# The last column block of 20 rows contracted as a block of 128, in a two-layer graph network on one core

## The chip, the cores and the metric

One Trainium2 chip, one of its cores. The metric is the device time of one execution in microseconds (us), the median of several runs. All data are float32. The engines have the names of the profile: PE is TensorE with its weight loads as PEld, DVE is VectorE, ACT is ScalarE, POOL is GpSimd, SP is SyncE, which here only issues DMAs.

## The reference

x is 2708 x 256, adj is 2708 x 2708 and sparse (about 0.3% filled, with a diagonal). Cut to what matters:

```
def layer0(x, adj, W, b):
    s = concatenate([x, adj @ x], axis=1)
    return layernorm(x + relu(s @ W + b))

def layer1(X, S, W1, W2, W3, U1, U2):
    R = (S + eye) / rowsum(S + eye)
    Xf = Xa = X; Z = 0
    for n in range(2):
        A  = top_p_attention(Xa, W1, W2, W3)   # softmax of q k^T, smallest set of mass 0.9, renormalized
        Xf = R @ Xf
        Xa = A @ Xa
        Z  = Z + Xf @ U1[n].T + Xa @ U2[n].T
    return layernorm(X + layernorm(X + Z))
```

2708 is 21 x 128 + 20, so a sum over all 2708 columns of adj, or of the attention matrix A, falls into 21 column blocks of 128 and a last one of 20.

## The kernel before

Rows are handled in NB = 22 blocks of P = 128, the last (EDGE = 21) with 20 rows. The order of instructions on every engine is that of the program text (a hand-written schedule); each engine takes its queue in that order. Tiles that the engines exchange are guarded by semaphores that the framework sets from the reads and writes of each region.

Layer 0 (L447 on). First y0 = x @ W[256:] is made for all blocks (L388 to L399) with a column of ones behind it at index D = 256, so that the row sum of adj comes along. Then for each row block m, `adj_product` (L247) adds up 22 products over the column blocks k in one PSUM tile: the stationary operand is a 128 x 128 piece of adj transposed, from the two loaded halves in `adj_of`, the moving one y0[:, k] of 257 columns. For k = 21 both have kw = 20 rows (partitions). The host sends adj as 128 x 128 blocks, filled with zeros beyond 2708. Then come x @ W[:256] (L462), the transposes of x1 (L438) and, every fourth block, the query and key projection (L426). On DVE the block has `name_columns` (L289), bias, relu and layernorm (L471 to L479) and, from block 16 on, rounds of list building (`lists.take`, L321 and L322).

`lists.end()` (L324 on) follows the loop of layer 0. DVE prepares a list, POOL stores it (L334), loads it back (L335), and DVE makes offsets of it (L339 to L341). POOL then sends seven scattering DMAs (L345), one after the other, and a load of the table ix (L348).

Next, attention step 1. Ahead of its loop, `begin1` makes the logits of blocks 0 to 2 (PE L507, ACT copy L514) with projections `u1_project` between (PE L651, ACT L654), `extract1` on DVE draws the 64 largest logits of a row (L570 to L579), `exps1` on ACT takes exponentials (L611, L613), and `finish1` on DVE finds and applies the threshold (L627 to L640). Then for each block t, in six groups of four column blocks, `turn` (L521) transposes the masked exponentials e to the tile wT (PE L527, ACT copies L530 and L533), and `products` (L553) multiplies wT with y (PE L564), one group later; y is x1 in step 1. The last group has two column blocks, k = 20 and k = 21, and k = 21 has 20 columns: a transpose of 20 columns, a separate ACT copy of 20 partitions (L533) and a product with 20 rows. Block 21, with 20 rows of its own, has its products in four column strips (L561), folded by `edge_sum` (L236).

Attention step 2 (from about 745 us) has the same `turn` and `products` with y = ya, which is Xa @ U2[1].T, made by `ya_pair` (L662) in pairs of blocks. Its row block 21 goes through `edge_product` (L536 on: PE L544, ACT L546, PE L550). Beside it run the sparse products of R (`r_units`, PE L749) with the gathered rows yg that POOL's indirect DMAs bring (`y_load`, L719), the threshold search on ACT (L966, L969) and DVE (L1023 to L1090), and the final layernorms.

e has NW = 2720 columns; those from 2708 on are set to zero at the start (L181). `y_room` (the tile yg) is 5416 columns wide; its first 4096 hold gathered rows, the next 1024 four spare tiles.

The forms to follow in the code are these:

```
nc.tensor.transpose(tr[:kw, k % 4, :p], e[:p, k * P:k * P + kw], ident[:p, :p])          # L527
nc.tensor.matmul(acc[:p, :D], lhsT=wT[:kw, k % 4, :p], rhs=y[:kw, k, :],                # L564
                 start=k == 0, stop=k == NB - 1)
nc.tensor.matmul(acc[:p, :n], lhsT=halves[k // KH][:kw, k % KH, :p], rhs=y[:kw, k, :n],  # L257
                 start=k == 0, stop=stop and k == NB - 1)
```

Of the kernel before, what the change touches and what calls it, by code (L numbers as in the profile page):

```python
# [20 lines left out]
P = 128  # L21
CH = 512
SEG = 170
NS = 16
# [14 lines left out]
CAP = 160  # L39
ML = 16  # L40
CW, CC = 128, 7


def chunks(N):
# [8 lines left out]
def gnn_two_layer_kernel(ctx: ExitStack, tc: tile.TileContext, N, xT_d, x_d, adj_d, w0_d, b0_d,  # L53
# [24 lines left out]
    nc = tc.nc  # L78
    D = x_d.shape[1]
    DA = w1_d.shape[1]  # L80
    NB = (N + P - 1) // P
    DC = D // P
    assert N % 2 == 0 and NB % 2 == 0 and N * 2.0 ** -15 < 0.09 and DC == 2 and DA == 64
    assert SEG * (NS - 1) + 8 <= N <= SEG * NS == SEG2 * NS2 and N >= SEG2 * (NS2 - 1) + 8
    assert NB == 3 * KS + 1 and CW == P and CAP % 8 == 0 and N < NB * P
    CHS = chunks(N)
    KH = NB // 2
# [61 lines left out]
def fast_path(ctx, tc, c, flags, fint, xT_d, x_d, w0_d, b0_d, w1_d, w2_d, w3_d, u1_d, u2_d, g_d, b_d):  # L149
    nc = tc.nc  # L150
    N, D, DA, NB, DC, KH, CHS, rows = c.N, c.D, c.DA, c.NB, c.DC, c.KH, c.CHS, c.rows
    ident = c.ident
# [94 lines left out]
    def adj_product(acc, m, y, n, stop):  # L247
        p = rows(m)
        halves = adj_of.pop(m)
        for k in range(NB):  # L250
            kw = rows(k)
            if m == EDGE:
                o = EW * (k % 4)
                nc.tensor.matmul(acc[o:o + p, :n], lhsT=halves[k // KH][:kw, k % KH, :p], rhs=y[:kw, k, :n],
                                 start=k < 4, stop=k >= NB - 4)
                continue
            nc.tensor.matmul(acc[:p, :n], lhsT=halves[k // KH][:kw, k % KH, :p], rhs=y[:kw, k, :n],  # L257
                             start=k == 0, stop=stop and k == NB - 1)


# [123 lines left out]
    adj_load(0, 0)  # L384
    adj_load(0, 1)
    y0 = big.tile([P, NB, D + 1], FP, tag="V", name="y0")
    nc.gpsimd.memset(y0[:, :, D:D + 1], 1.0)
    for t in range(NB):  # L388
        p = rows(t)
# [99 lines left out]
    YW = 2 * (CC + 1) * D  # L489
    yg = y_room[:, :YW].rearrange("p (s c d) -> p s c d", s=2, d=D)  # L490
    spares = [y_room[:, YW + D * i:YW + D * (i + 1)] for i in range(4)]
    lists = Lists(ML, NB, flags[:, NF - 2:], yg[:, 1].rearrange("p c d -> p (c d)"))
    lists.turn()
    x1_transpose(NB - 1)
# [23 lines left out]
    NG = (NB + 3) // 4  # L518
    before = []

    def turn(t, g, y, acc, e):  # L521
        p = rows(t)
        ks = range(4 * g, min(NB, 4 * g + 4))
        tr = ps_tr()
        for k in ks:
            kw = rows(k)
            nc.tensor.transpose(tr[:kw, k % 4, :p], e[:p, k * P:k * P + kw], ident[:p, :p])  # L527
        wT = work.tile([P, 4, P], FP, tag="wT", name="wT", bufs=3)
        full = sum(rows(k) == P for k in ks)
        nc.scalar.copy(wT[:, :full, :p], tr[:, :full, :p])  # L530
        if full < len(ks):
            kw = rows(ks[full])
            nc.scalar.copy(wT[:kw, full, :p], tr[:kw, full, :p])  # L533
        before.append((p, ks, wT, y, acc))

    def edge_product(y, acc, e):  # L536

        p = rows(EDGE)
        tr = ps_tr().rearrange("p k i -> p (k i)")[:, :NB * p].rearrange("p (k i) -> p k i", i=p)
        wT = work.tile([P, 4, P], FP, tag="wT", name="wT", bufs=3)  # L540
        wT = wT.rearrange("p k i -> p (k i)")[:, :NB * p].rearrange("p (k i) -> p k i", i=p)
        for k in [NB - 1] + list(range(NB - 1)):
            kw = rows(k)
            nc.tensor.transpose(tr[:kw, k, :], e[:p, k * P:k * P + kw], ident[:p, :p])  # L544
        for a, b, kw in ((0, NB - 1, P), (NB - 1, NB, rows(NB - 1))):
            nc.scalar.copy(wT[:kw, a:b, :], tr[:kw, a:b, :])  # L546
        for k in range(NB):
            kw = rows(k)
            o = EW * (k % 4)
            nc.tensor.matmul(acc[o:o + p, :D], lhsT=wT[:kw, k, :], rhs=y[:kw, k, :],  # L550
                             start=k < 4, stop=k >= NB - 4)

    def products(keep):  # L553

        if len(before) > keep:
            p, ks, wT, y, acc = before.pop(0)
            for k in ks:
                kw = rows(k)
                if p < P:
                    o = EW * (k % 4)  # L560
                    nc.tensor.matmul(acc[o:o + p, :D], lhsT=wT[:kw, k % 4, :p], rhs=y[:kw, k, :],  # L561
                                     start=k < 4, stop=k >= NB - 4)
                    continue
                nc.tensor.matmul(acc[:p, :D], lhsT=wT[:kw, k % 4, :p], rhs=y[:kw, k, :],  # L564
                                 start=k == 0, stop=k == NB - 1)

    def seg_max(dst, src, p, step, width):
# [94 lines left out]
    def ya_pair():  # L662
# [11 lines left out]
        if rows(t0 + 1) == P:  # L674
            nc.scalar.copy(ya[:, t0:t0 + 2, :], pz)
            return
        for s in range(2):
            nc.scalar.copy(ya[:rows(t0 + s), t0 + s, :], pz[:rows(t0 + s), s, :])

    def step1_out(t, acc, ra):  # L680

# [215 lines left out]
    for t in range(NB):  # L897
# [6 lines left out]
        for g in range(NG):  # L904
# [16 lines left out]
            if g == 2:  # L921
                if t + 3 < NB:
                    extract1(t + 3)
                if t < 9:
                    lists.take(2 * t + 2, 2 * t + 4)
                if t == 8:
                    lists.end()
            if (t, g) in at:
                adj_gather(at[t, g])
                stores += [(NG * t + g + i, at[t, g], i - 4) for i in (4, 5)]  # L930
# [804 lines left out]
```

## Time and profile before

| | |
|---|---|
| median of 3 runs | 1295.33 us (1294.3 to 1296.72) |
| the profiled execution | 1291.2 us; span of its instructions 1289.4 us; mean granted PE clock 0.986 |
| PE busy | 1226.3 us, 95% |
| DVE busy | 973.9 us, 76% |
| ACT busy | 735.5 us, 57% |
| POOL busy | 635.9 us, 49% |
| L564, L257 matmuls (passes) | 924 on x and 924 on ya at L564, 924 at L257 |
| ACT copies at L530 (all forms) | 258, 132.1 us |

Every float32 product shows as two passes, each with a weight load (PEld), so 924 is 2 x 21 x 22. A form such as 20*128 20x256 gives the rows and columns of the stationary operand, then partitions and columns of what moves. A PE row of the timeline ends late, since the ends of pipelined matmuls are modelled: the distance from start to start is what a pass costs. "Idle before" with a releaser says what ended the wait; "issue" means that the profile shows nothing that it waited for.

The chain of work that ended last is 79% PE, 8% DVE, 7% ACT, 3% DMA and 2% POOL.

### The profile page before, as it was taken

To read this page: it belongs to the slowest core of one execution; us is meant where nothing else is said; L and a number is where in the kernel's file an instruction comes from. 1 tells how busy PE (TensorE), PEld (TensorE's weight loads), DVE (VectorE), ACT (ScalarE), POOL (GpSimd) and SP (SyncE) were. 2 spreads that over 40 slices of the span, in tenths; PEclk is the share of its full clock that TensorE was granted. 3 is DMA by queue.
4 is the path that set the end of the run, shared out by engine and by line. 5 is a ranking of instruction groups with operands and counts; after the bars stand their busy time and mean duration, and the time that the engine had idled before them with its cause. 6 is when DMAs were issued, how large, how long until landed. Compare 5 with 4: busy or idle time off the path is not lost.

```text
span 1289.4 us, 18741 instructions
## 1 busy us (share of the span) xinstructions
PE 1226.3 (95%) x5764; PEld 888.1 (69%) x5764; DVE 973.9 (76%) x3252; ACT 735.5 (57%) x1337; POOL 635.9 (49%) x594
## 2 busy tenths in 40 slices
PE   8999999979899999999999987999999999999885
PEld 6878777843477777777777555777766777767664
DVE  2445545884999997977872179889888999999886
ACT  2000110125456656556655488887888989989822
POOL 1000000003475452577756058878874878888860
PEclk9999999999999999999999988999999999999998
DMA  7455445423322210122224244565563545565451
GB/s 196 152 193 170 143 149 168 149 90 107 121 82 83 72 57 28 43 88 91 93 85 100 63 149 150 178 189 177 180 154 118 179 155 154 165 195 158 145 139 39
DMA packets 101703, 165.99 MB, mean 129 GB/s; under 512 B 17362, under 2 KB 74070, under 8 KB 101594
## 3 DMA queue, kind: packets, MB, share of 16 engines
q1 hardware_dynamic: 75308, 108.65, 26.0%
q0 software_dynamic: 20544, 51.17, 14.3%
q10 hardware_dynamic: 5742, 4.89, 1.3%
q8 instruction: 48, 0.79, 0.2%
q14 instruction: 61, 0.50, 0.1%
HBM read 130.74 MB, written 33.90 MB: 128 GB/s over the span
## 4 chain that ended last, share of the span: by engine, by line
PE 79%; DVE 8%; ACT 7%; DMA 3%; POOL 2%; issue 2%; ACTq 0%; POOLq 0%; DVEq 0%
PE acc L564 27%; PE acc L257 16%; PE lg L507 9%; PE misc L749 8%; PE tr L527 7%; PE acc L651 2%; DMA yg<-v_d,ix 2%; PE acc L462 2%; PE misc L392 2%; PE misc L426 2%; PE acc L672 2%; ACT e L966 2%; PE misc L699 1%; DVE e L1088 1%; ACT e L844 1%
## 5 line engine op out<-in xcount | busy, mean ns | idle before, releaser
L530 ACT COPY wT<-tr 128x512 f32<-128x512 f32 (+2 forms) x258 | 132.1, 519 | 208.7 <-PE tr L527 208.7
L564 PE MATMUL acc<-x,wT 128*128 128x256 f32 (+1 forms) x924 | 230.5, 388 | 0.0
L564 PE MATMUL acc<-ya,wT 128*128 128x256 f32 (+1 forms) x924 | 227.1, 385 | 0.0
L719 POOL DMA_INDIRECT yg<-v_d,ix x154 | 194.8, 1265 | 59.6 <-issue 22.6
L564 PEld LDWEIGHTS acc<-x,wT 128*128 128x128 f32 (+1 forms) x924 | 165.2, 189 | 71.0 <-issue 37.4
L719 POOL DMA_INDIRECT yg<-yf_d,ix x154 | 188.2, 1222 | 48.3 <-issue 22.5
L257 PE MATMUL acc<-y,adj_t 128*128 128x257 f32 (+1 forms) x924 | 208.4, 381 | 0.0
L564 PEld LDWEIGHTS acc<-ya,wT 128*128 128x128 f32 (+1 forms) x924 | 170.2, 190 | 44.4 <-issue 24.0
L749 PE MATMUL misc<-yg,adj_t 128*128 128x256 f32 (+1 forms) x704 | 183.7, 394 | 14.9 <-DMA yg<-v_d,ix 5.9
L367 POOL DMA_INDIRECT adj_t<-in_adj,ix x154 | 171.3, 1112 | 52.0 <-issue 41.8
L257 PEld LDWEIGHTS acc<-y,adj_t 128*128 128x128 f32 (+1 forms) x924 | 171.8, 189 | 32.7 <-issue 8.9
L749 PEld LDWEIGHTS misc<-yg,adj_t 128*128 128x128 f32 (+1 forms) x704 | 123.6, 189 | 67.6 <-issue 23.4
L507 PE MATMUL lg<-k,q 64*128 64x512 f32 (+3 forms) x528 | 149.5, 594 | 13.7 <-ACT e L848 7.0
L527 PE MATMUL tr<-ident,e 128*128 128x128 f32 (+2 forms) x946 | 147.1, 274 | 3.1 <-DVE e L1088 2.0
L527 PEld LDWEIGHTS tr<-ident,e 128*128 128x128 f32 (+2 forms) x946 | 112.2, 138 | 44.8 <-issue 16.4
L334 POOL DMA_DIRECT2D part_d<-e x1 | 0.6, 573 | 285.6 <-DVE e L333 285.6
L439 ACT COPY x1T<-tr 128x256 f32<-128x256 f32 (+1 forms) x22 | 8.0, 364 | 186.6 <-PE tr L438 186.6
L966 ACT ACTIVATE e<-e,st 128x2708 f32<-128x2708 f32 (+1 forms) x43 | 113.5, 2639 | 0.1
L969 ACT ACTIVATE e<-e,st 128x2708 f32<-128x2708 f32 (+1 forms) x42 | 110.9, 2641 | 0.1
L570 DVE MAX8 cand<-e 128x8 f32<-128x170 f32 (+1 forms) x352 | 87.2, 318 | 26.7 <-ACT e L514 26.7
L1030 DVE MAX8 cand<-w 128x8 f32<-128x170 f32 (+1 forms) x352 | 94.2, 321 | 0.0
L1083 DVE MATCH_REPLACE8 w<-part,e 128x680 f32<-128x680 f32 (+1 forms) x88 | 74.3, 851 | 0.0
(238 smaller groups left out, 1696.4 us busy)
## 6 DMA issues: line engine op xcount, KB each, us to landing
adj_t<-in_adj SPq DMA_DIRECT2D x44, 704.0 KB
adj_t<-adjc_d SPq DMA_DIRECT2D x44, 448.0 KB
adjc_d<-adj_t SPq DMA_DIRECT2D x22, 256.0 KB
base<-za_d SPq DMA_DIRECT2D x40, 128.0 KB
adjc_d<-adj_t SPq DMA_DIRECT2D x22, 192.0 KB
xt<-in_x ACTq DMA_DIRECT2D x21, 128.0 KB
x_d<-x SPq DMA_DIRECT2D x21, 128.0 KB
x1b_d<-xb SPq DMA_DIRECT2D x21, 128.0 KB
```

The source lines that it names most:

```text
L257: nc.tensor.matmul(acc[:p, :n], lhsT=halves[k // KH][:kw, k % KH, :p], rhs=y[:kw, k, :n], start=k == 0, stop=stop and k == NB - 1)
L367: nc.gpsimd.indirect_dma_start(out=a[:CW, i, :], out_offset=None, in_=adj_rows, in_offset=bass.IndirectOffsetOnAxis(ap=ix[:CW, m, i:i + 1] ...
L507: nc.tensor.matmul(lg[:p, h, :b - a], lhsT=q[o, t * P:t * P + p], rhs=keys[s][o, i, :b - a], start=True, stop=True)
L527: nc.tensor.transpose(tr[:kw, k % 4, :p], e[:p, k * P:k * P + kw], ident[:p, :p])
L530: nc.scalar.copy(wT[:, :full, :p], tr[:, :full, :p])
L564: nc.tensor.matmul(acc[:p, :D], lhsT=wT[:kw, k % 4, :p], rhs=y[:kw, k, :], start=k == 0, stop=k == NB - 1)
L570: nc.vector.max(dst[:p, i * 8:(i + 1) * 8], src[:p, i * step:i * step + w])
L719: nc.gpsimd.indirect_dma_start(out=y[:CW, i, :], out_offset=None, in_=rows_d, in_offset=bass.IndirectOffsetOnAxis(ap=ix[:CW, m, i:i + 1], ...
L749: nc.tensor.matmul(acc[:p, :D], lhsT=a[:kw, k, :p], rhs=y[:kw, k, :], start=k == 0, stop=k == CC)
L966: nc.scalar.activation(scr[:b.p, :N], e, AF.Relu, bias=b.nz, scale=b.l[k], accum_out=b.relu)
L969: nc.scalar.activation(scr[:b.p, :N], e, AF.Sign, bias=b.nz, scale=b.l[k], accum_out=b.sign)
L1030: nc.vector.max(b.cand[:p, 8 * i:8 * i + 8], low[:p, SEG2 * i:SEG2 * (i + 1)])
```

## The change

In layer 0 and in the attention the last column block is contracted over 128 rows, like all others.

- Layer 0: kw goes away. adj's rows beyond 20 in the last block are zero as sent. A memset on POOL makes all of y0[:, 21, :D] zero before the 20 rows are written.
- Attention: for k = 21, `columns` takes the last 128 of e's 2720 columns, 2592 to 2719. The first 96 (AT) of these belong to block 20 and so are taken twice; the next 20 are block 21's, the last 12 are zero. The moving operand has its 20 rows at partitions 96 to 115 and zeros elsewhere: in step 1 a new tile x1_edge, a piece of y_room, in step 2 ya[:, 21, :].
- x1_edge is set to zero by POOL and its 20 rows copied by DVE, after `lists.end()`. ya[:, 21, :] is set to zero by POOL in block 2 of step 1.
- The ACT copies of the last group are one copy of 256 columns in place of two, and one in place of two in `edge_product`, which also transposes the column blocks in their order.

```diff
+AT = 96
@@ adj_product
         for k in range(NB):
-            kw = rows(k)
             if m == EDGE:
                 o = EW * (k % 4)
-                nc.tensor.matmul(acc[o:o + p, :n], lhsT=halves[k // KH][:kw, k % KH, :p], rhs=y[:kw, k, :n],
+                nc.tensor.matmul(acc[o:o + p, :n], lhsT=halves[k // KH][:, k % KH, :p], rhs=y[:, k, :n],
                                  start=k < 4, stop=k >= NB - 4)
                 continue
-            nc.tensor.matmul(acc[:p, :n], lhsT=halves[k // KH][:kw, k % KH, :p], rhs=y[:kw, k, :n],
+            nc.tensor.matmul(acc[:p, :n], lhsT=halves[k // KH][:, k % KH, :p], rhs=y[:, k, :n],
@@ before layer 0
     y0 = big.tile([P, NB, D + 1], FP, tag="V", name="y0")
+    nc.gpsimd.memset(y0[:, NB - 1, :D], 0.0)
     nc.gpsimd.memset(y0[:, :, D:D + 1], 1.0)
@@ after lists.end()
     spares = [y_room[:, YW + D * i:YW + D * (i + 1)] for i in range(4)]
+    x1_edge = y_room[:, YW + 4 * D:YW + 5 * D]
+    nc.gpsimd.memset(x1_edge, 0.0)
+    nc.vector.tensor_copy(x1_edge[AT:AT + rows(EDGE)], x1[:rows(EDGE), EDGE, :])
     lists = Lists(ML, NB, flags[:, NF - 2:], yg[:, 1].rearrange("p c d -> p (c d)"))
@@ attention
+    def columns(e, k):
+
+        a = min(k * P, NW - P)
+        return e[:, a:a + P]
+
+    def part_y(y, k):
+        return y[:, k, :] if k < NB - 1 or y is ya else x1_edge
+
@@ turn
         for k in ks:
-            kw = rows(k)
-            nc.tensor.transpose(tr[:kw, k % 4, :p], e[:p, k * P:k * P + kw], ident[:p, :p])
+            nc.tensor.transpose(tr[:, k % 4, :p], columns(e[:p], k), ident[:p, :p])
         wT = work.tile([P, 4, P], FP, tag="wT", name="wT", bufs=3)
-        full = sum(rows(k) == P for k in ks)
-        nc.scalar.copy(wT[:, :full, :p], tr[:, :full, :p])
-        if full < len(ks):
-            kw = rows(ks[full])
-            nc.scalar.copy(wT[:kw, full, :p], tr[:kw, full, :p])
+        nc.scalar.copy(wT[:, :len(ks), :p], tr[:, :len(ks), :p])
@@ edge_product
-        for k in [NB - 1] + list(range(NB - 1)):
-            kw = rows(k)
-            nc.tensor.transpose(tr[:kw, k, :], e[:p, k * P:k * P + kw], ident[:p, :p])
-        for a, b, kw in ((0, NB - 1, P), (NB - 1, NB, rows(NB - 1))):
-            nc.scalar.copy(wT[:kw, a:b, :], tr[:kw, a:b, :])
         for k in range(NB):
-            kw = rows(k)
+            nc.tensor.transpose(tr[:, k, :], columns(e[:p], k), ident[:p, :p])
+        nc.scalar.copy(wT, tr)
+        for k in range(NB):
             o = EW * (k % 4)
-            nc.tensor.matmul(acc[o:o + p, :D], lhsT=wT[:kw, k, :], rhs=y[:kw, k, :],
+            nc.tensor.matmul(acc[o:o + p, :D], lhsT=wT[:, k, :], rhs=part_y(y, k),
@@ products
-                kw = rows(k)
                 if p < P:
                     o = EW * (k % 4)
-                    nc.tensor.matmul(acc[o:o + p, :D], lhsT=wT[:kw, k % 4, :p], rhs=y[:kw, k, :],
+                    nc.tensor.matmul(acc[o:o + p, :D], lhsT=wT[:, k % 4, :p], rhs=part_y(y, k),
                                      start=k < 4, stop=k >= NB - 4)
                     continue
-                nc.tensor.matmul(acc[:p, :D], lhsT=wT[:kw, k % 4, :p], rhs=y[:kw, k, :],
+                nc.tensor.matmul(acc[:p, :D], lhsT=wT[:, k % 4, :p], rhs=part_y(y, k),
@@ ya_pair
-        for s in range(2):
-            nc.scalar.copy(ya[:rows(t0 + s), t0 + s, :], pz[:rows(t0 + s), s, :])
+        nc.scalar.copy(ya[:, t0, :], pz[:, 0, :])
+        p = rows(t0 + 1)
+        nc.scalar.copy(ya[AT:AT + p, t0 + 1, :], pz[:p, 1, :])
@@ loop of step 1
+            if (t, g) == (2, 0):
+                nc.gpsimd.memset(ya[:, NB - 1, :], 0.0)
```

More of the change, by code (lines that the diff above doesn't have):

```diff
@@ L84, in gnn_two_layer_kernel @@
     assert SEG * (NS - 1) + 8 <= N <= SEG * NS == SEG2 * NS2 and N >= SEG2 * (NS2 - 1) + 8
+    assert SEG * NS - P == (NB - 1) * P - AT and AT + N - (NB - 1) * P <= P
     assert NB == 3 * KS + 1 and CW == P and CAP % 8 == 0 and N < NB * P
```

## The prediction

> **What bounds the kernel now.** I read the page first, then the stretches, then the timeline around one 20-row step in each stage, then the start of the first attention step.
>
> ```profile
> span 1289.4 us, 18741 instructions
> ...
> PE 1226.3 (95%) x5764; PEld 888.1 (69%) x5764; DVE 973.9 (76%) x3252; ACT 735.5 (57%) x1337; POOL 635.9 (49%) x594
> ...
> PE acc L564 27%; PE acc L257 16%; PE lg L507 9%; PE misc L749 8%; PE tr L527 7%; PE acc L651 2%; DMA yg<-v_d,ix 2%; PE acc L462 2%; PE misc L392 2%; PE misc L426 2%; PE acc L672 2%; ACT e L966 2%; PE misc L699 1%; DVE e L1088 1%; ACT e L844 1%
> ```
>
> PE is busy 95% of the span and L564 and L257, the two lines that hold the 20-row products, are 43% of the chain that ended last. But the share is an average; what a PE saving is worth must be read stage by stage. The stretches below are one row block each: layer 0, attention step 1, then four of attention step 2 (columns: stretch, length, busy us and count of each engine, granted clock, DMA share, GB/s).
>
> ```profile
> 39.50:50.50 11.00, 11.00 (x52) 9.06 (x51) 6.15 (x15) 1.58 (x2) 0.00 (x0) 1.00 0.52 175
> 468.65:486.19 17.54, 17.54 (x90) 12.71 (x89) 15.95 (x59) 10.56 (x20) 9.08 (x10) 1.00 0.22 68
> 806.86:830.65 23.79, 23.79 (x116) 17.99 (x115) 21.36 (x73) 19.93 (x33) 18.91 (x17) 1.00 0.55 172
> 1018.31:1041.23 22.92, 22.92 (x111) 17.22 (x111) 21.00 (x75) 20.33 (x35) 18.35 (x16) 1.00 0.56 178
> 1087.60:1111.00 23.40, 23.34 (x111) 17.03 (x110) 23.09 (x75) 22.26 (x40) 19.55 (x17) 1.00 0.55 174
> 1206.00:1230.00 24.00, 21.29 (x96) 16.93 (x96) 20.68 (x68) 18.11 (x30) 19.72 (x19) 0.93 0.49 147
> ```
>
> Layer 0 and step 1 are PE-bound: PE fills the whole stretch, and in step 1 the blocks repeat every 17.54 us to the hundredth. Step 2 is PE-bound at its start, DVE-bound near 1090 (23.09 of 23.40; the waits of DVE in 1087 to 1135 are an empty list) and held by transfers near 1210 (PE waits 5.9 us for yg<-v_d,ix between 1064 and 1258).
>
> One 20-row step in layer 0, PE and its weight loads:
>
> ```profile
> 37.46 1.01 PE L257 MATMUL acc<-y,adj_t 128*128 128x257 f32 x3
> 38.40 0.48 PE L462 MATMUL acc<-e,xT 128*128 128x256 f32 x1
> ```
> ```profile
> 37.77 0.29 PEld L257 LDWEIGHTS acc<-y,adj_t 20*128 20x128 f32 x2 [0.33 <-issue]
> 38.40 0.19 PEld L462 LDWEIGHTS acc<-e,xT 128*128 128x128 f32 x1 [0.33 <-issue]
> ```
>
> Each f32 product is two passes. The last full pass starts at 37.46, the two 20-row passes begin at 37.77, and the next full product starts at 38.40: 0.94 us from full to full over three intervals. The two idles of 0.33 us, ended by nothing but issue, are the array emptying before and after.
>
> **What the Trainium skill says.** "TensorEngine Tiling (Array Packing)", Key Properties: "Changing tiling mode (not just tile) drains the TensorE", and 32-row contractions are another mode than 128. The trace agrees: 0.31 us into the 20-row pass, 0.32 between its two, 0.305 out, against 0.216 between full passes. "TensorE: Matmul & The Clock Gate", section on LDWEIGHTS, says a load's time follows the columns, not the contraction depth, so 128 rows should not load dearer; here a full load shows 0.19 us, wholly under the 0.216 rhythm. Its head table calls the queues of ScalarE, VectorE and GpSimd strict FIFO; the trace shows POOL and DVE in program order throughout. Its Part 1 says a PE idle for about 3.4 us falls to half clock: here the clock is 0.50 from 338.6 to 342.0, after an idle of 3.91 us.
>
> **The change part by part.**
>
> *The 20-row pair becomes a 128-row pair.* Its columns and moving width are unchanged, so it should run at the rhythm of its neighbours: 3 x 0.216 = 0.648 instead of 0.934 us, 0.286 saved each time. Where the other engines follow PE the block shortens by this.
>
> *Layer 0:* 21 blocks x 0.286 = **6.0 us saved**. DVE holds 16 list rounds of about 1.25 us in the last five full blocks and still waits for PE 0.45, 0.86 and 0.55 us at L471 in three of them, so it does not become the bound. The edge block starts on the memset at L172 behind DVE; its own shorter step is hidden by DVE's L289 (3.13 us): 0.
>
> *Attention step 1:* 21 x 0.286 = **6.0**, period 17.54 to 17.25. DVE is busy 15.95 and waits about 0.83 per block on ACT's L514, itself led by PE, so it needs 16.7: below 17.25. The transposes of the last group cost the same with 128 as with 20 columns (start to start 0.109 both). ACT has one 128x256 copy (L439 of this size: 0.37) for copies of 0.27 and 0.25; ACT is not late here (10.56 of 17.54): 0. The edge block's last product changes from 20 to 128 rows too: about **0.3**.
>
> *Attention step 2:* the same 0.286 in 21 blocks, but kept only where PE leads. I count seven blocks to 956 us, three between 995 and 1064, one at 1164, one at 1258: 12 x 0.286 = **3.4**. Lost: the block near 980 (PE waits for ACT and DVE, some 3.7 us in 978 to 995), those of 1064 to 1160 (DVE is next, with no wait left), those of 1185 to 1240 (yg arrives last). Bounds 2.0 and 6.0.
>
> *Tail:* the last edge product loses one ACT copy (0.25) and one mode change among 44 passes: about **0.5** on the path.
>
> *The added zero rows.* y0's memset on POOL is the size of L276's (0.30) and lies at 6.6 us, with y0's last copy due at 26 us: 0. ya's memset goes to POOL in block 2, and ya is first written after 720 us: 0; the gather queue behind it shifts by 0.3 in a stage where POOL is busy 9.08 of 17.54. x1_edge is different: its memset is on POOL and its copy on DVE *waits for it*, and the built program's order puts the memset behind the list scatter and the load of ix, and the copy ahead of block 0's MAX8s at L570. POOL, DVE and ACT there now:
>
> ```profile
> 316.11 1.24 POOL L348 DMA_DIRECT2D ix<-list_d  x1 [1.40 <-DMA list_d<-e,to]
> 317.35 0.11 POOL L584 MEMSET xs<- 128x1 f32 x1
> ```
> ```profile
> 297.92 3.86 DVE L570 MAX8 cand<-e 128x8 f32<-128x170 f32 x16
> ```
> ```profile
> 320.36 0.21 DVE L627 TENSOR_SCALAR sc<-z 128x1 f32<-128x1 f32 x1 [10.73 <-ACT e L613]
> ```
> ```profile
> 317.17 0.35 ACT L611 ACTIVATE srt<-srt,nmax 128x65 f32<-128x65 f32 x1
> ...
> 334.38 0.35 ACT L611 ACTIVATE srt<-srt,nmax 128x65 f32<-128x65 f32 x1 [2.99 <-DVE srt L577]
> ```
>
> POOL sends seven scatters, each waiting for the one before to land, and reaches 317.35. Then memset 0.30 and copy 0.4 (L479 of 20x256: 0.41) end at about 318.05 on this clock, so block 0's extraction, which ran 297.92 to 307.29, runs 318.05 to 327.4. That is a hold of 20.1 us on DVE. Queued behind it: the extraction, two list rounds, finish1(0) at L627. Waiting for those: ACT's L611 and, behind it in ACT's queue, the copies that free PSUM for PE. L611 moves from 317.17 to 327.4, **10.2 us**. The other 10 are covered by the 10.73 us that DVE now idles ahead of L627. What follows, finish1(0), extraction of block 1, L611 at 334.38, block 0's turns at 343.45, is on the chain that ended last and moves with it. Bounds: not below 9.8 (copy for nothing), since the queue orders exclude passing; above, PE's longer idle may cost one or two half-clock stretches of 3.4 us, 1.7 us of work each, and ACT's slack of 2.99 ahead of the second L611 covers most: up to 12. I take 10.2.
>
> *Sum:* -6.0 - 6.0 - 0.3 - 3.4 - 0.5 + 10.2 = **-6.0 us**. The profiled execution took 1291.2 us (span 1289.4), so it would be 1285.2. The median of the runs is 1295.33, 4.1 above it, so the median after is **1289.3**. A measurement of this kernel tells about 0.2% (2.6 us) from no change.
>
> **Rivals.**
>
> *A, the forecast:* -6.0, own range 1286 to 1292.5 from the bounds above. Chance 0.68.
>
> *B, the hold is covered:* POOL's scatters are quicker than now, or the wait costs only its own length. Then -16.2: 1279.1. For it: DVE has 10.73 us of idle there. Against it: that idle is already subtracted, and POOL's rounds are paced by landings, which nothing in the change shortens. 0.10.
>
> *C, slower: the hold goes through whole.* The place is DVE's L627; if the 10.73 us of idle there is no cover, because POOL's chain then ends later, the price is about 20.1, and -16.2 + 20.1 = +3.9: 1299.2. It decides when the uncovered part exceeds 16.2 us, that is when the memset starts 6 us later than 317.35 in this clock. For it: each scatter round takes 2.2 to 3.2 us and DMA times vary. Against it: fewer transfers compete while DVE and ACT stand. 0.08.
>
> *D, no measurable change:* step 2 gives its gain back altogether (DVE and the yg transfers bound more of it than I count), and 1 us of half clock comes on top: -6.0 + 3.4 + 1 = -1.6: 1293.7. For it: DVE is busy 21 to 23 of each 23. Against it: PE fills its stretches to 956. 0.14.
>
> Faster is A and B, 0.78; same D, 0.14; slower C, 0.08. The range takes in A and D with their bounds, 1285 to 1294.5, and leaves out B and C, 0.18.
>
> **What would show it.** Layer 0's blocks should come every 10.75 us instead of 11.03, step 1's every 17.25, with no 0.33 us idles at 20-row loads. DVE should show one long idle, near 19 us, ahead of a copy of x1, released by POOL; the turns of block 0 should start about 4 us later than 343.45 (10.2 - 6.0). Step 2 should shrink by 2 to 4 us and not by 6. I am wrong if the 128-row pair does not run at 0.216 a pass, if the DVE hold is short, or if step 1's blocks stay at 17.54 because DVE leads.

## The result, and the profile after

| | before | after |
|---|---|---|
| median of 8 runs | 1295.24 us (1294.3 to 1297.57) | 1285.13 us (1282.82 to 1289.59) |
| ratio after / before | | 0.9926, 95% interval 0.9909 to 0.9942 |
| profiled execution | 1291.2 us, span 1289.4 | 1285.77 us, span 1284.0 |

The medians differ by 10.1 us, the profiled executions by 5.4. The profiled execution of before was quicker than each of its eight timed runs, that of after lies 0.6 us above its median. The prediction took the step from trace to median (4.1 us) to be the same for both kernels; that is where 4.7 of the 10.1 us come from, and it is taken up again below.

In after the lines stand a little lower in the file: L257 is now L258, L462 L464, L507 L512, L527 L539, L530 L541, L564 L568, L570 L574, L611 L615, L627 L631, L749 L754. L495 and L496 are the memset and the copy of x1_edge.

The page of after:

```profile
span 1284.0 us, 18686 instructions
...
PE 1209.3 (94%) x5764; PEld 902.1 (70%) x5764; DVE 973.6 (76%) x3253; ACT 733.8 (57%) x1293; POOL 628.1 (49%) x597
...
PE acc L568 24%; PE acc L258 16%; PE lg L512 9%; PE misc L754 6%; PE tr L539 6%; DMA yg<-yf_d,ix 3%; DMA yg<-v_d,ix 2%; PE acc L655 2%; POOL yg L724 2%; PE misc L394 2%; DVE e L1095 2%; PE misc L428 2%; PE acc L676 2%; ACT e L973 2%; PE misc L704 1%
```

PE has as many instructions as before (5764) and is busy 17 us less; ACT has 44 copies fewer, for 1.7 us. The span fell by 5.4, so more than half of what PE lost came back as waiting. Most of that is the transition of the table below (+10.13). The chain shows another part: a gather, yg<-yf_d, which had no share among the first fifteen lines, now has 3%.

Both traces were cut at the same events: the first pass of layer 0's first block, the first pass of the attention's products, and the last pass of the products of block 20 of layer 0, block 20 of step 1, block 0 of step 2 and block 20 of step 2. So the row block of 20 rows of layer 0 lies in the transition, and the edge stretch holds block 21 of step 1, the way to step 2 and its block 0.

| us | before | after | difference | predicted |
|---|---|---|---|---|
| up to layer 0 | 28.45 | 29.55 | +1.10 | 0 |
| layer 0 | 239.92 | 231.95 | -7.97 | -6.0 |
| transition to the first product | 78.97 | 89.10 | +10.13 | +10.2 |
| step 1, blocks 0 to 20 | 364.62 | 357.58 | -7.04 | -6.0 |
| edge of step 1, block 0 of step 2 | 100.31 | 100.17 | -0.14 | -0.3 |
| step 2, blocks 1 to 20 | 457.86 | 456.39 | -1.47 | -3.4 |
| tail | 19.23 | 19.26 | +0.03 | -0.5 |
| span | 1289.36 | 1284.00 | -5.36 | -6.0 |

Stretches of one row block each in after: layer 0, step 1, then four of step 2 (stretch, length, busy us and count of PE, PEld, DVE, ACT and POOL, granted clock, DMA share, GB/s):

```profile
39.50:50.15 10.65, 10.65 (x51) 9.28 (x50) 6.03 (x14) 0.29 (x1) 0.00 (x0) 1.00 0.54 180
468.65:485.85 17.20, 17.20 (x90) 12.89 (x90) 15.96 (x59) 10.53 (x20) 9.10 (x10) 1.00 0.22 69
832.72:856.32 23.60, 23.60 (x115) 18.07 (x114) 20.43 (x70) 19.91 (x33) 18.98 (x16) 1.00 0.59 174
904.45:928.85 24.40, 23.97 (x115) 18.03 (x114) 20.03 (x69) 19.89 (x33) 19.53 (x17) 1.00 0.61 179
1019.93:1042.51 22.58, 22.58 (x111) 17.44 (x110) 20.89 (x75) 20.29 (x35) 14.16 (x13) 1.00 0.56 176
1088.29:1111.72 23.43, 23.05 (x111) 17.28 (x110) 23.12 (x76) 22.25 (x39) 19.45 (x18) 1.00 0.57 175
```

Layer 0 and step 1 are still full on PE, with shorter blocks (10.65 from 11.04, 17.20 from 17.54). The stretch at 1019 is 22.58 from 22.92, full on PE as before. The one at 1088 was 23.43 in before too: DVE is busy 23.12 of it and ACT 22.25, and PE's new wait of 0.3 us ends at ACT's copy to wT. And at 904 there is a block of 24.40 where before had 23.78 for the same block: PE shows 0.43 us of idle there.

The 20-row step itself. Weight loads of the end of a layer 0 block in after:

```profile
37.48 1.50 PEld L258 LDWEIGHTS acc<-y,adj_t 128*128 128x128 f32 x7
39.00 0.84 PEld L464 LDWEIGHTS acc<-e,xT 128*128 128x128 f32 x4
```

The 20-row rows and both idles of 0.33 us are gone; 39.00 follows the seven loads at the same rhythm of 0.216 us.

The hold at the start of the attention, POOL, DVE and ACT of after (x1_edge is a piece of the tile yg and shows under that name):

```profile
308.85 1.24 POOL L349 DMA_DIRECT2D ix<-list_d  x1 [1.39 <-DMA list_d<-e,to]
310.08 0.33 POOL L495 MEMSET yg<- 128x256 f32 x1
310.33 0.11 POOL L588 MEMSET xs<- 128x1 f32 x1
```
```profile
290.35 0.21 DVE L342 SCALAR_TENSOR_TENSOR to<-run,before_m,e 16x7 int32<-16x7 f32 x1
310.44 0.56 DVE L496 COPY yg<-x 20x256 f32<-20x256 f32 x1 [19.89 <-POOL xs L588]
311.01 3.88 DVE L574 MAX8 cand<-e 128x8 f32<-128x170 f32 x16
...
323.64 0.21 DVE L631 TENSOR_SCALAR sc<-z 128x1 f32<-128x1 f32 x1 [0.90 <-ACT e L617]
```
```profile
320.44 0.35 ACT L615 ACTIVATE srt<-srt,nmax 128x65 f32<-128x65 f32 x1 [10.28 <-DVE srt L581]
...
337.64 0.35 ACT L615 ACTIVATE srt<-srt,nmax 128x65 f32<-128x65 f32 x1 [1.24 <-DVE srt L581]
```

DVE stands 19.89 us in front of the copy. The releaser reads L588, but that is the 0.11 us instruction behind the memset in POOL's queue; releasers are inferred from semaphore events, and the thing waited for is the memset at 310.08. The idle of 10.73 us ahead of the threshold (now L631) has shrunk to 0.90: this is the cover being used up. What remains shows on ACT as 10.28 us ahead of L615, and the slack of 2.99 us ahead of the second L615 is down to 1.24.

### The profile page after: what moved, and what is told of

Its sections match the earlier page's. It is cut to its first block, busy times and chain, and to the rows that moved or that the text cites. A ratio compares the mean times of both kernels' runs of the same rounds, so it can differ in the third digit from the quotient of the medians.

```text
span 1284.0 us, 18686 instructions
## 1 busy us (share of the span) xinstructions
PE 1209.3 (94%) x5764; PEld 902.1 (70%) x5764; DVE 973.6 (76%) x3253; ACT 733.8 (57%) x1293; POOL 628.1 (49%) x597
## 4 chain that ended last, share of the span: by engine, by line
PE 72%; DVE 9%; ACT 7%; DMA 6%; POOL 3%; issue 2%; ACTq 0%; POOLq 0%; DVEq 0%
PE acc L568 24%; PE acc L258 16%; PE lg L512 9%; PE misc L754 6%; PE tr L539 6%; DMA yg<-yf_d,ix 3%; DMA yg<-v_d,ix 2%; PE acc L655 2%; POOL yg L724 2%; PE misc L394 2%; DVE e L1095 2%; PE misc L428 2%; PE acc L676 2%; ACT e L973 2%; PE misc L704 1%
## 5 line engine op out<-in xcount | busy, mean ns | idle before, releaser
L541 ACT COPY wT<-tr 128x512 f32<-128x512 f32 (+2 forms) x258 | 136.4, 536 | 202.4 <-PE tr L539 202.1
L568 PE MATMUL acc<-ya,wT 128*128 128x256 f32 x924 | 224.0, 384 | 0.0
L568 PE MATMUL acc<-x,wT 128*128 128x256 f32 x882 | 217.4, 386 | 0.0
L258 PE MATMUL acc<-y,adj_t 128*128 128x257 f32 x924 | 204.4, 379 | 0.0
L568 PEld LDWEIGHTS acc<-x,wT 128*128 128x128 f32 x882 | 159.0, 190 | 63.7 <-issue 30.4
L568 PEld LDWEIGHTS acc<-ya,wT 128*128 128x128 f32 x924 | 172.8, 192 | 38.6 <-issue 17.0
L754 PE MATMUL misc<-yg,adj_t 128*128 128x256 f32 (+1 forms) x704 | 185.5, 395 | 15.1 <-DMA yg<-yf_d,ix 6.1
L258 PEld LDWEIGHTS acc<-y,adj_t 128*128 128x128 f32 x924 | 173.7, 189 | 26.8 <-issue 1.9
L368 POOL DMA_INDIRECT adj_t<-in_adj,ix x154 | 165.3, 1073 | 50.8 <-issue 40.1
L512 PE MATMUL lg<-k,q 64*128 64x512 f32 (+3 forms) x528 | 150.6, 598 | 24.3 <-ACT e L519 10.9
L754 PEld LDWEIGHTS misc<-yg,adj_t 128*128 128x128 f32 (+1 forms) x704 | 123.0, 189 | 69.5 <-issue 27.9
L539 PE MATMUL tr<-ident,e 128*128 128x128 f32 (+1 forms) x946 | 145.9, 273 | 4.7 <-ACT wT L541 2.7
L539 PEld LDWEIGHTS tr<-ident,e 128*128 128x128 f32 (+1 forms) x946 | 118.3, 142 | 38.0 <-ACT wT L541 6.4
L574 DVE MAX8 cand<-e 128x8 f32<-128x170 f32 (+1 forms) x352 | 87.1, 318 | 21.4 <-ACT e L519 21.4
L512 PEld LDWEIGHTS lg<-k,q 64*128 64x128 f32 (+1 forms) x528 | 39.3, 183 | 56.3 <-issue 20.6
```

What stands on the lines that cost most here:

```text
L258: nc.tensor.matmul(acc[:p, :n], lhsT=halves[k // KH][:, k % KH, :p], rhs=y[:, k, :n], start=k == 0, stop=stop and k == NB - 1)
L368: nc.gpsimd.indirect_dma_start(out=a[:CW, i, :], out_offset=None, in_=adj_rows, in_offset=bass.IndirectOffsetOnAxis(ap=ix[:CW, m, i:i + 1] ...
L512: nc.tensor.matmul(lg[:p, h, :b - a], lhsT=q[o, t * P:t * P + p], rhs=keys[s][o, i, :b - a], start=True, stop=True)
L539: nc.tensor.transpose(tr[:, k % 4, :p], columns(e[:p], k), ident[:p, :p])
L541: nc.scalar.copy(wT[:, :len(ks), :p], tr[:, :len(ks), :p])
L568: nc.tensor.matmul(acc[:p, :D], lhsT=wT[:, k % 4, :p], rhs=part_y(y, k), start=k == 0, stop=k == NB - 1)
```

## The experiments

Two theories. *Mine:* each 20-row product costs PE the emptying of the array around it; three stages get that back as far as PE leads, and a POOL memset behind seven scatters takes ten of it away at one place. *Rivals:* the hold costs little, and the saving is smaller than thought, so that the same sum comes out; the price of a 20-row product is that of a short tile as such, not of a change of form; step 2 loses its gain to DVE and not to the transfers.

Experiments 1 to 4 ran on one chip and 5 to 7 on another; these took 1341.7 and 1345.88 us for the kernel before. Their traces have longer blocks in both steps of the attention. In that of experiment 1, ACT's copies to wT wait 13.2 us in step 1 for "issue" and 12.3 for "remote"; where these stops come from was not found. Experiments 8 to 10 ran on a third chip and 11 on a fourth, which took 1294.33 and 1296.43; their traces, with those of before and after, are called quiet below. Ratios are always against the kernel before on the same chip, with a 95% interval behind them.

### 1. The kernel before again

No edit.

> The kernel before, unchanged, for a second trace of it. The two profiled executions differ by 5.4 us (1289.4 to 1284.0) and the medians by 10.1 (1295.24 to 1285.13). Theory: the profiled execution of before was a quick one, so this one has a span near 1293.5, with layer 0 and step 1 equal to the first trace within 0.2 us and the difference in attention step 2, where transfers bound it. Rival: the span is again 1289 to 1290, and the 4.7 us lie outside the span or between chips. Ratio to before 1.000.

1341.04 us, ratio 0.9998 (0.9973 to 1.0023), span 1338.3. On this chip the question could not be put, since everything is 45 us longer. It serves as the trace of before beside experiments 2 to 4: layer 0 239.91, transition 80.19, step 1 384.99, step 2 472.03.

### 2. The zeroing put ahead of the lists

After, with the memset of x1_edge issued before the scatters that POOL sends in `lists.end()`:

```diff
-    lists.end()
     y_room = ...
-    yg = ...
-    spares = ...
     x1_edge = y_room[:, YW + 4 * D:YW + 5 * D]
     nc.gpsimd.memset(x1_edge, 0.0)
+    lists.end()
+    yg = ...
+    spares = ...
     nc.vector.tensor_copy(x1_edge[AT:AT + rows(EDGE)], x1[:rows(EDGE), EDGE, :])
```

> The changed kernel with the memset of x1_edge (and the tile it is a part of) put ahead of the list building, so that POOL does it before its scatters; the copy on DVE stays where it is. Theory: the hold of DVE goes, 10.6 us earlier first turn of block 0, and step 2 gives nothing of it back: 1274.5 us (ratio to before 0.984), range 1272 to 1278. Rival 1, the hold is covered: 1285. Rival 2, the later part of step 2 is paced by POOL's gathers from a fixed start: half is given back, 1280.

1318.72 us, ratio 0.9831 (0.98 to 0.9862). Transition 78.63 us against 80.19 of before on this chip; layer 0 231.95 as in after. The hold is a matter of the memset's place in POOL's queue, and the early place shows no cost. Experiments 7 and 11 repeat this beside after and on a quieter chip.

### 3. The hold alone

Before, with a memset and a copy that nothing reads:

```diff
+AT = 96
     spares = ...
+    x1_edge = y_room[:, YW + 4 * D:YW + 5 * D]
+    nc.gpsimd.memset(x1_edge, 0.0)
+    nc.vector.tensor_copy(x1_edge[AT:AT + rows(EDGE)], x1[:rows(EDGE), EDGE, :])
```

> The kernel before with only the memset of x1_edge and the copy of 20 rows added at the place of the change; nothing reads x1_edge. Theory: DVE stands about 19.9 us, first turn of block 0 later by 10.6 us, 1305.9 us (ratio 1.008). Rival, covered by the 10.7 us idle of DVE: 1295. Rival, it goes through whole: 1315.

DVE around the copy, and its wait there (engine and line, what was waited for: us in total, times, longest):

```profile
318.19 0.56 DVE L495 COPY yg<-x 20x256 f32<-20x256 f32 x1 [19.71 <-POOL xs L588]
```
```profile
DVE yg L495 <- POOL xs L588: 19.7, 1, 19.7
```

The same standing of DVE, with no product changed. The transition is 87.82 us against 80.19, +7.6. The time is 1344.83 us, ratio 1.0019 (1.0 to 1.0039), that is 0 to 5 us: less than the trace's +7.6, and the expected 1.008 is refused on this chip. In this one trace step 1 and its edge are 4.4 us shorter than in experiment 1, and step 2 is 3.9 longer, without any edit there, so the runs of this chip scatter by as much as the effect. It shows the mechanism; the price is better taken from the pairs below.

### 4. Layer 0 alone

Before, with this only:

```diff
+    nc.gpsimd.memset(y0[:, NB - 1, :D], 0.0)
@@ adj_product
-            kw = rows(k)
-                ... lhsT=halves[k // KH][:kw, k % KH, :p], rhs=y[:kw, k, :n],
+                ... lhsT=halves[k // KH][:, k % KH, :p], rhs=y[:, k, :n],
```

> Only the layer 0 part of the change. Theory from the trace after: 0.388 us a block, 21 blocks, 8.1 us: 1287.1 (ratio 0.9937). The prediction's size, 0.286 a block: 6.0, 1289.2. Rival: step 2 gives it back or the start of layer 0 is later by 1 us because of the memset of y0: 1288 to 1290 with the block period still 10.65.

Layer 0 takes 231.95 us, to the hundredth what after takes, from 239.91; step 1 stays at 384.88 (384.99). 1332.92 us, ratio 0.9936 (0.9913 to 0.9959): -8.6 us, with the trace's -7.96 well inside the interval. Layer 0's blocks save 0.388 each, not 0.286. That the gain reaches the end whole fits the time, but the interval (5.5 to 11.7 us) takes in the 6.0 of the prediction as well; the trace alone tells the two apart.

### 5. Step 1 alone

Early zeroing as in experiment 2, with layer 0 and step 2 as in before; `turn`, `products` and the edge choose the new form only for y = x1:

```diff
+        if y is not ya:
+            for k in ks:
+                nc.tensor.transpose(tr[:, k % 4, :p], columns(e[:p], k), ident[:p, :p])
...
+                new = y is not ya
+                kw = P if new else rows(k)
+                r = part_y(y, k) if new else y[:kw, k, :]
```

> Only the part of attention step 1, with the memset of x1_edge early. Theory from the trace after: 0.343 us a block (17.54 to 17.20), 21 blocks, 7.2 us, and 0.4 at the edge block: ratio 0.994. The prediction's size: 0.286, 6.3 us with the edge, 0.995. Rival, step 2 gives it back: no change.

1336.51 us, ratio 0.994 (0.9922 to 0.9958): -8.1 us. Layer 0 is back at 239.91; step 1 375.51 against 384.99 in the trace of before on a like chip, though the stops of this chip lie in that stage and differ from run to run.

### 6. Step 2 alone

The converse: the new forms only where y is ya, no x1_edge at all.

```diff
+        if y is ya:
...
+                new = y is ya
```

> Only the part of attention step 2 (ya with its rows at 96 to 115, the last group of 128 columns, the edge product); no x1_edge, so no hold. The prediction: 3.4 us and 0.5 at the end, 0.997. Theory from the trace after: PE's 0.34 us a block turns into a wait for yg<-yf_d and later for DVE and yg<-v_d, so that 1 to 1.5 us stay: 0.999. Rival: all 21 blocks keep it, 7.2 us: 0.9945.

1343.26 us, ratio 0.9988 (0.9966 to 1.001): -1.6 us with an interval from -4.6 to +1.3. By itself it does not tell 1.5 from the predicted 3.4, but it rules out the 6 us and more that step 2 would give if PE led all through it. Experiments 4, 5 and 6 add up to -18.3 us.

### 7. After and the early zeroing, side by side

After itself, and the kernel of experiment 2 again, on the chip of experiments 5 and 6.

> The changed kernel itself, to be compared with the next three on one chip, since the chip of the first four runs gave 1341 us for the kernel before. Theory: ratio to before 0.9926 on a chip like the first, layer 0 at 10.65 us a block, step 1 at 17.20, DVE standing 19.9 us ahead of the copy of x1. Rival: on a chip with more stalls the gain is another, 0.99 or lower.

> The changed kernel with the memset of x1_edge ahead of the list building, once more, beside the changed kernel on the same chip. Theory: 10.6 us less than the changed kernel (0.8%), ratio to before near 0.9845. Rival, the hold is partly covered or given back in step 2: 3 to 6 us less.

After: 1333.49 us, ratio 0.9906 (0.9871 to 0.9941), transition 87.94 us. Early zeroing: 1326.27, ratio 0.9856 (0.9819 to 0.9892), transition 78.85. So the hold is 9.1 us in the traces and 7.2 by the medians, whose intervals overlap.

### 8. How many rows make the product dear

Before, with layer 0's last block contracted over 20 rows in row blocks 0 to 6, over 64 in 7 to 13, over 96 in 14 to 20 (adj and y0 hold zeros there):

```diff
+            kw = rows(k) if k < NB - 1 else (rows(k), 64, 96)[m // 7]
```

> The kernel before with layer 0's last column block contracted over 20 rows in row blocks 0 to 6, over 64 in 7 to 13 and over 96 in 14 to 20 (the added rows are zeros). Theory, the price is that of a change of the array's row mode, not of few rows: blocks 0 to 6 repeat every 11.04 us, 7 to 13 too (64 rows are another mode than 128), 14 to 20 every 10.65[...]. Rival, any contraction below 128 rows pays: all at 11.04. Rival, only 32-row tiles pay: 64 rows at 10.65.

The block takes 11.04 us with 20 rows, 11.04 with 64 and 10.65 with 96. The weight loads at three such places, one in each third:

```profile
38.30 0.29 PEld L257 LDWEIGHTS acc<-y,adj_t 20*128 20x128 f32 x2 [0.33 <-issue]
```
```profile
164.37 0.30 PEld L257 LDWEIGHTS acc<-y,adj_t 64*128 64x128 f32 x2 [0.33 <-issue]
165.00 0.73 PEld L463 LDWEIGHTS acc<-e,xT 128*128 128x128 f32 x4 [0.33 <-issue]
```
```profile
213.96 7.37 PEld L257 LDWEIGHTS acc<-y,adj_t 128*128 128x128 f32 x34
221.36 0.84 PEld L463 LDWEIGHTS acc<-e,xT 128*128 128x128 f32 x4
```

At 64 rows the same two idles of 0.33 stand before and after the pair, and its two passes start 0.322 us apart as those of 20 rows do. At 96 rows there is no idle, and the pair appears merged in the row of the full loads. So the price goes neither with the rows nor with being short of 128: it falls on 20 and 64 rows alike and not on 96. That is what a change between tiling modes would do. The Trainium skill, "TensorEngine Tiling (Array Packing)", Tiling Modes, lists tiles of 128, 64 and 32 rows; the measurement fits it, with 64 rows in another mode than 128 and 96 carried in that of 128. Whether 20 and 64 rows are two modes or one it does not tell. Nor does it exclude a price of each product of 64 rows or fewer by itself, since none here follows another such product; that the full pass behind the pair is late too (0.320 us to the next start in place of 0.216, at 20 and at 64 rows) speaks for the change.

### 9. One gather fewer, in before

Before, with six of the seven gathers of a row block in R @ y. The seventh product takes the sixth piece again, so PE has the same work and the kernel leaves out a part of R @ y:

```diff
-        for i in range(CC):
+        for i in range(CC - 1):
-            ... rhs=y[:kw, k, :], start=k == 0, stop=k == CC)
+            ... rhs=y[:kw, k - (k == CC - 1), :], start=k == 0, stop=k == CC)
```

> The kernel before with six of the seven gathers of yg for each row block; the product of the seventh piece is kept but takes the sixth piece again, so PE's work is unchanged and a part of R @ y is left out. It is the base for the next kernel. Theory: POOL has a seventh less to send in step 2, PE's waits for yg shrink, the blocks before the middle of step 2 are 23.78 us as before, in all 5 to 15 us less than the kernel before. Rival, POOL's gathers bound nothing: within 3 us of it.

### 10. One gather fewer, with step 2's part

The same with the edit of experiment 6.

> The step 2 part of the change alone, on top of six gathers of seven (the same part of R @ y is left out). Theory: with POOL's gathers out of the way the first seven blocks of step 2 are 23.44 us each, and the part is worth 4 to 5 us against the kernel with six gathers (blocks bound by DVE near the middle still keep nothing), against 1.6 with seven. Rival, it is not the gathers that take the gain: again 1 to 2 us.

Experiment 9: 1284.66 us, ratio 0.9934 (0.9916 to 0.9952). Experiment 10: 1282.61, ratio 0.9903 (0.9889 to 0.9917). Two stretches of step 2 in each, first 9, then 10, one row block long (columns as above):

```profile
861.42:885.20 23.78, 23.78 (x115) 17.98 (x114) 20.13 (x69) 19.93 (x34) 17.18 (x15) 1.00 0.59 178
1092.50:1115.70 23.20, 23.19 (x112) 17.14 (x110) 22.45 (x79) 22.30 (x40) 18.72 (x16) 1.00 0.55 171
```
```profile
864.42:887.86 23.44, 23.44 (x115) 18.20 (x114) 20.13 (x70) 19.89 (x33) 17.87 (x15) 1.00 0.58 180
1092.77:1115.96 23.19, 22.86 (x111) 17.36 (x110) 22.44 (x79) 22.25 (x39) 18.72 (x17) 1.00 0.54 170
```

With one gather fewer the early blocks go from 23.78 to 23.44 one and all (six blocks of 23.78 or 23.79 become six of 23.44 or 23.45), and the three of 22.92 become 22.58: 0.34 each, what step 1 gains. The block near 1092 does not move, 23.20 and 23.19; only PE's share of it falls, 23.19 to 22.86, so it is waiting 0.33 more, and this wait ends at ACT's copy to wT. DVE is busy 22.44 us there and ACT 22.25; which of the two leads was not separated.

The step 2 part as a whole: -2.1 us by the traces (446.39 to 444.29) and by the medians, about -4 by the ratios, whose intervals overlap; so neither the expected 4 to 5 nor the rival's 1 to 2 is refused. Ten blocks (these nine and the seventh) give 3.4 and the short one at the end another 0.34, but the last two full blocks take 1.7 us longer. PE's waits on DVE's last column work, from 745 us on, first experiment 9, then 10:

```profile
PE tr L527 <- DVE e L1088: 3.7, 3, 2.7
```
```profile
PE tr L537 <- DVE e L1107: 6.0, 3, 3.1
```

PE arrives earlier and waits longer: 2.3 us more, for the same DVE. One thing is not the same in the two traces: the edge stretch ahead took 104.83 us in experiment 10 and 100.35 in 9, without a difference of the edit that explains 4.5 us. So the gathers of experiment 10 had more time before the first full blocks, and how much that helped these was not separated.

### 11. Early zeroing on a quieter chip

The kernel of experiment 2 a third time, on a chip that takes 1296.43 us for before.

> The changed kernel with the memset of x1_edge early, a third time, for a chip that gives the kernel before near 1295 us, where the changed kernel stood at 0.9926. Theory: the hold costs 10.1 to 10.6 us there and nothing after it gives that back, so the ratio is 0.9845 (1275 us at 1295). Rival, the hold is worth only the 3 to 7 us that the slower chips showed: 0.987 to 0.990.

1276.84 us, ratio 0.9859 (0.984 to 0.9878), span 1273.9: the fastest of the versions that leave nothing out. The expected 0.9845 lies in the interval, the rival's 0.987 in it too, and 0.990 outside. DVE at the end of `lists.end()` and ACT's first L615:

```profile
290.46 0.21 DVE L342 SCALAR_TENSOR_TENSOR to<-run,before_m,e 16x7 int32<-16x7 f32 x1
290.69 0.28 DVE L496 COPY yg<-x 20x256 f32<-20x256 f32 x1
290.99 3.88 DVE L574 MAX8 cand<-e 128x8 f32<-128x170 f32 x16
```
```profile
309.70 0.35 ACT L615 ACTIVATE srt<-srt,nmax 128x65 f32<-128x65 f32 x1
```

No idle ahead of the copy, the extraction 20 us earlier than in after, and L615 at 309.70 in place of 320.44. The transition is 78.80 us against 89.10: 10.3. The median lies 8.3 us below that of after, the ratios (0.9859 and 0.9926) put 8.7 us between them. Layer 0 is 231.95 and step 1 357.57, as in after; the edge stretch is 102.52 and step 2 454.44.

## Why the prediction was right, and where not

*The hold of DVE, +10.2: right in place, and in this pair in size.* The memset starts where it was put, behind the load of ix; DVE stands 19.89 us (20.1 forecast), the 10.73 us ahead of the threshold give all but 0.90 as cover, and the transition grows by 10.13. PE, idle for longer, pays half clock there: after 10.37 us of idle the granted clock is 0.50 from 324.55 to 326.50, and the first four logits passes take 2.08 us, against 1.12 for the four that follow at full clock.

```profile
324.55 2.08 PE L512 MATMUL lg<-k,q 64*128 64x512 f32 x4 [10.37 <-ACT e L519]
...
330.98 1.12 PE L512 MATMUL lg<-k,q 64*128 64x512 f32 x4
```

ACT's slack ahead of the second L615 pays for that, as the upper bound said: it falls by 1.75 us, and nothing is left over in the transition. Rival B (covered) and rival C (whole) are both refused by the 0.90: the cover is there, and it is not larger.

The size is partly luck. In the three pairs of traces that differ by the hold alone the transition grows by 10.30 us (experiment 11 to after), 9.09 (experiment 7) and 7.63 (experiments 1 and 3), 9.0 on average, and two of the three lie below the bound of 9.8. A part of the difference lies in the last eight passes of PE before block 0's turns, in after and then in experiment 7's run of after:

```profile
341.33 5.46 PE L655 MATMUL acc<-u,x1T 128*128 128x512 f32 x8 [2.16 <-ACT v_out L658]
```
```profile
341.79 3.81 PE L655 MATMUL acc<-u,x1T 128*128 128x512 f32 x8 [0.81 <-ACT v_out L658]
```

In before they take 5.46 us too, behind the idle of 3.91, with the clock at 0.50 for 3.4 us. With the hold in experiments 3 and 7 PE idles only 0.81 us ahead of them, the clock stays at 1.00, and 1.65 us are won back. The prediction had counted half clock as a cost of the hold alone.

*What a 20-row product costs: right in mechanism, mis-sized.* The prediction had "3 x 0.216 = 0.648 instead of 0.934 us, 0.286 saved each time". Measured are 0.388 per block in layer 0 (11.04 to 10.65) and 0.343 in step 1 (17.54 to 17.20). The working counted the passes up to the next full product and left out one late pass behind it, which the trace of before shows: the second pass of the product behind the pair starts 0.320 us after its first, in place of 0.216. So the four passes of x @ W[:256] in layer 0 take 1.13 us in before and 1.02 in after, of the same form, first before, then after:

```profile
38.40 1.13 PE L462 MATMUL acc<-e,xT 128*128 128x256 f32 x4
```
```profile
39.22 1.02 PE L464 MATMUL acc<-e,xT 128*128 128x256 f32 x4
```

In step 1 of before, the four transposes that follow a 20-row product against four that follow full ones:

```profile
607.26 0.65 PE L527 MATMUL tr<-ident,e 128*128 128x128 f32 x4
...
610.74 0.60 PE L527 MATMUL tr<-ident,e 128*128 128x128 f32 x4
```

Start to start the late pass is 0.104 us in layer 0 and 0.055 in step 1. 0.286 + 0.104 and 0.286 + 0.055 come within 0.002 of the measured savings. So layer 0 gave 2.0 us and step 1 1.0 us more than forecast; experiment 4 has layer 0's part in isolation, and the traces of after and of experiment 11 have step 1's to the hundredth. The Trainium skill, "TensorEngine Tiling (Array Packing)", Key Properties, says that changing the tiling mode drains TensorE; experiment 8 agrees, 64 rows paying like 20 and 96 nothing.

*Step 2, -3.4: not reached in this pair.* The sign that was named, 2 to 4 us, was missed: -1.47. "I count seven blocks to 956 us, three between 995 and 1064, one at 1164, one at 1258." The later ones came out. The three went from 22.92 to 22.58 each, and the blocks of 23.20, 23.43 and 23.70 us kept nothing, in both traces. Blocks 8 to 20 together took 290.20 us in before and 289.96 in experiment 8, which has the same step 2; they took 288.25 in after and 288.30 in experiment 11: 1.7 to 2.0 saved, where five blocks of 0.286 make 1.4. What failed in this pair is the early part, where the prediction took a stretch that PE fills for one that PE leads; it is taken here as blocks 1 to 7: they sum to 167.66 us before and 168.14 after, where 2.0 should have been saved. Weight loads' waits from 800 to 953 us, before and then after (line, what was waited for: us in total, times, longest):

```profile
PEld misc L749 <- issue: 9.1, 12, 0.8
...
PEld misc L749 <- DMA base<-v_d: 0.8, 1, 0.8
```
```profile
PEld misc L754 <- issue: 9.1, 12, 0.8
...
PEld misc L754 <- DMA yg<-yf_d,ix: 4.7, 7, 1.1
```

In before no load waits for a gathered row in this window; in after seven do, 4.7 us in all. PE filled its stretches, as I read it, but the gathers came only just in time. That they are what lengthens these blocks is shown by experiments 9 and 10: with six gathers in place of seven, blocks 1 to 7 take 165.82 us in the old form and 163.42 in the new, shorter than in any quiet trace of the same form with seven. That PE was full could not tell this; the distance between each landing and its use would have.

That the new form as such meets the gathers, and so keeps nothing, is not shown. The other two quiet traces with seven gathers have 169.00 us for blocks 1 to 7 in the old form (experiment 8) and 166.14 in the new (experiment 11, where four of the blocks take 23.44). Their loads wait for gathered rows as well, first experiment 8, then 11, in these blocks:

```profile
PEld misc L750 <- DMA yg<-yf_d,ix: 2.9, 4, 1.0
```
```profile
PEld misc L754 <- DMA yg<-yf_d,ix: 3.4, 5, 1.3
```

In the same blocks it is 1.0 us in before and 5.5 in after. Two traces of one form differ by 1.3 to 2.0 us, as much as the forecast saving. By the medians step 2 is open too: -1.6 with an interval that takes in -3.4 (experiment 6).

*Tail, -0.5: not seen* (+0.03). In the traces the tail is near 19.2 or near 21 us in either version, so half a microsecond can't be told there. *The edge of step 1* shows -0.14 for -0.3, in a stretch that differs by 2.4 us between after and experiment 11, so this can't be told either. *y0's memset, 0:* the +1.1 us up to layer 0 is scatter; that stretch takes 28.45 to 29.91 in the traces, 29.07 in experiment 3, which has no such memset, and 29.11 in experiment 11, which has it. *ACT's copies, 0:* 44 fewer, 1.7 us less busy. In step 2 PE's transposes wait longer for ACT's copies to wT, 2.7 us in six waits (after, 783 to 1260 us) against 1.1 in two (before, 786 to 1266). So part of what PE saves ends in these waits.

*The sum.* On the stages the errors nearly cancel: layer 0 and step 1 gave 3.0 more, step 2 and the tail 2.5 less. Trace against trace the forecast -6.0 stands beside -5.4. By the medians the change is -10.1 (ratio: -7.5 to -11.8), and the forecast of 1289.3 is 4 us too high. The measured 1285.13 lies below the range of A itself (1286 to 1292.5) and only 0.13 us inside the whole range of 1285 to 1294.5; that it lies inside is luck. Part by part the medians say -8.6 (layer 0), -8.1 (step 1) and -1.6 (step 2), together -18.3, which is what experiment 11 measures for all three without the hold (0.9859 of 1296.43, -18.3); after lacks 8.7 of that. The traces say -8.0, -7.0, -1.5 and +10.1. The first three lie in the intervals of experiments 4 to 6, and all four lie on the side of the smaller gain. That the trace of before was a quick execution accounts for a part of it: 1291.2 us against 1294.3 for the quickest timed run, and a trace of a kernel equal to it outside layer 0 (experiment 8) shows step 2 at 458.96 and the tail at 20.93, 2.8 us more for both. For the hold, the 8.7 of the medians is close to the 9.0 that the three pairs of traces give on average. Where the rest lies was not found. Experiment 1 was meant for it and fell on a chip that takes 45 us longer.

## What to carry to other kernels

Look for contractions of 64 rows or fewer among ones of 128: the trace shows them as pairs of short idles of PE's weight loads that end on nothing, and padding them to the full height is paid in zero rows. Count what is saved over a whole block period, since a pass behind the switch is late as well. This holds for products that stand alone. The logits of this kernel contract 64 rows too, but two at a time: their passes start 0.006 us apart (before, at 607.85 us), and padding them was not tried. And give padding memsets a place in a queue that is empty at that time: the same 0.33 us memset cost about nine microseconds behind seven scatters and nothing that shows ahead of them.

## What the runs showed of the hardware that was not expected

- A float32 product of 20 rows costs one late pass beyond the switch itself: 0.104 us on a following product of 256 columns, 0.055 on following transposes. In all 0.39 or 0.34 us for each such product, against the 0.43 us that the two passes of a full one take.
- 64 rows pay as much as 20, 96 rows as little as 128 (experiment 8).
- One of seven gathers per row block is worth about 9 us in this kernel (experiment 9: ratio 0.9934, 6 to 11 us, and step 2 at 446.39 against 457.86 and 458.96), though POOL was never busy for a whole stretch and PE showed hardly a wait for them in the early blocks of before (0.2 us).
- A longer idle of PE does not always leave more half clock in its way. With the hold, in two traces of three, the stretch at 0.50 ahead of block 0's turns was gone (eight passes in 3.81 us in place of 5.46), after an earlier stretch at 0.50 of 13.65 us in place of 10.24, of which PE was idle for about half.
